# Binding the first masks of the divisors behind a projection's last exponential, and turning one adjacency mask a tile earlier, in a four-layer graph network

## The chip, the cores and the metric

The kernel runs on one core of a Trainium2 chip. The metric is the device time of one execution in microseconds (us). The engines are TensorE (PE, with its weight loads as PEld), VectorE (DVE), ScalarE (ACT), GpSimd (POOL) and SyncE (SP), which here only issues DMAs.

## The reference

N = 2708 nodes with 512 features pass four layers over one adjacency matrix `adj` (2708 x 2708, some 2% ones). Every layer adds its output to its input and normalizes each row (layer norm). Cut to what matters:

```python
# layer 0: only the first 64 neighbours of each row count
keep   = (adj > 0) & (cumsum(adj > 0, axis=1) <= 64)
xj     = leaky_relu((keep @ x) / max(keep.sum(1), 1) @ W_nb.T + b_nb)
x      = layernorm(x + leaky_relu(x @ W_line.T + b_line) + where(keep.any(1), xj, 0))
# layer 1: mean over all neighbours, joined with the node itself
x      = layernorm(x + relu(concat([x @ W_self + b_self, mean_nb(x) @ W_nb + b_nb]) @ W_comb + b_comb))
# layer 2: graph attention, 8 heads of 64
Wh     = einsum('ni,hio->hno', x, W)
e      = leaky_relu(f1[:, :, None] + f2[:, None, :], 0.2)   # f1, f2: Wh against two vectors per head
h      = softmax(where(adj > 0, e, -9e15)) @ Wh
x      = layernorm(x + heads_side_by_side(h))
# layer 3: 8 heads as in layer 2 with elu, then one head of 512 with elu, then two linear layers
```

## The kernel before, in words

The rows are cut into NT = 22 tiles of 128; the last has 20 rows. `maskT` holds the transposed adjacency of all tiles in fp8 and stays in SBUF.

**First stage (layer 0's products, L297 to L339).** A loop over t = 0 to 21 makes two products of each tile of x: one with `wnT` (kept in two parts, yH and yL) and one with `wlT` (to `r0_dram`). Between them lies the work on the adjacency: mask i is loaded by GpSimd's queue (`load_mask`, L257), counted on ScalarE (`count`, L262), cut to the first 64 on VectorE (`place`, L268 and L271), and turned (`turn`): 22 transposes on TensorE (L280) and copies with Sign to `maskT` on ScalarE (L284). Fourteen of the 22 masks (HERE = 14) are treated in this stage; one is counted in each of a part of the steps, the last at t = 18. TensorE's order in this stage is written out by `pe()`, which chains each instruction behind the one before it. `while turned < counted - (...)` sets how far the turning lags behind the counting.

**Second stage (keep @ x, L343 on).** For groups of tiles, `kept` makes kT from `maskT` on ScalarE (L350, two buffers), and TensorE multiplies (L477). The other eight masks (14 to 21) are treated beside it by the generator `other_masks`: each is loaded into one of two rooms, `spare` or `w`, and the room of mask 14 (`spare`) lies where the masks of the first stage lay. The count of mask 14 is issued on ScalarE behind the seventh kT.

**Projection (`project`, p2 and p3).** For each tile: TensorE multiplies (L642), VectorE takes columns b and dcol (L649, L647), ScalarE makes `ecol` and `ucol` by Exp (L663, L664; for the last tile in two halves, L655 and L657), VectorE scales the product into R2 (R, L671; L660 for the last tile), and `keep_v` of the tile before turns b by a transpose (L621), takes Exp (`vrow`, L622) and stores it to `v_dram`. In the steps 16 to 19 `first` makes the attention's first four e (L718), two tiles for two heads. At the end VectorE splits ecol and ucol into bf16 parts (L581 to L585, L684, L687).

**Attention (`heads_attention`, a2 and a3).** For each block of 11 tiles and pair of heads (a run, r), over the tiles j in `order`: VectorE makes e (five buffers), ScalarE makes the mask c of e in fp8 by Sigmoid (`above`, L745, eleven buffers), TensorE multiplies e (L910), and every four tiles it multiplies the masks for the divisors (`divisors`, L814). TensorE's order here is written out by `pe()` too. The accumulators `po` lie in PSUM space that the projection used.

Outside of the orders written out, a scheduler orders each engine's queue from the dependencies, so that ScalarE may take a mask between two steps of the projection. `tc.issue_after(ins)` binds the instructions traced inside it behind `ins` where they are on the engine of `ins`; it adds no wait between engines.

Of the kernel before, what the change touches and what calls it, by code (L numbers as in the profile page):

```python
# [13 lines left out]
AF = mybir.ActivationFunctionType  # L14
# [8 lines left out]
ALPHA = 0.2  # L23
# [7 lines left out]
def kernel(  # L31
# [9 lines left out]
    nc = tc.nc  # L41
    N = x.shape[0]
    NT = -(-N // P)
# [6 lines left out]
    def rows(t):  # L50
        return min(P, N - t * P)
# [101 lines left out]
    def weight():  # L153
        return weight_tile().rearrange("p k a c -> p (k a c)")[:, :KD * D].rearrange("p (k c) -> p k c", k=KD)

    def early(first, n, make):

        made = {}

        def get(i, **how):  # L160
            for j in range(len(made), min(i + first + 1, n)):
                made[j] = make(j, **how)
            return made[i]
        return get
# [36 lines left out]
    with ExitStack() as phase:  # L201
# [26 lines left out]
        def keep_y(t, n, pm):  # L228
            highs[t] = nc.scalar.copy(yH[:n, t, :], pm[:n])  # L229
            return nc.vector.tensor_sub(yL[:n, t, :], pm[:n], yH[:n, t, :].bitcast(F32))  # L230
# [57 lines left out]
        def rows_of(src):  # L288
            return early(2, NT, lambda t: fetched(src, t, rows(t)))

        with ExitStack() as ph:
            st = ph.enter_context(tc.tile_pool(name="l0a", bufs=1))
            wnT, wlT = weight(), weight2
            room = [maskT[:, G + k, :4 * D].bitcast(F32) for k in range(2 * KD)]

            xs = rows_of(x)
            xTs = early(0, NT, lambda t, order=as_it_comes: transposed(ahead, ps_tr, xs(t), rows(t), "xT", order))

            transpose_weight(room[:KD], ps_tr, wnT, l0_w_nb)
            lows = {}
            for t in range(2):
                xT = xTs(t, order=pe)
                lows[t] = keep_y(t, P, product(xT, P, wnT, 0, pe))
            transpose_weight(room[KD:], ps_tr, wlT, l0_w_line)
            b_line = bias(bcast(l0_b_line, D))
            masks = early(1, HERE, lambda i: load_mask(i, st.tile([P, N], BF16, name="m", bufs=3)))
            masks(0)
            nc.gpsimd.memset(maskT[:, NT - 1, :], 0.0)  # L310
            nc.gpsimd.memset(maskT[:, :, N:], 0.0)
            counted = turned = 0
            for t in range(NT):
                n = rows(t)
                if t > 1:
                    lows[t] = keep_y(t, n, product(xTs(t, order=pe), n, wnT, 0, pe))
                xT = xTs(t)
                if t + 1 < NT:
                    xTs(t + 1, order=pe)
                while turned < counted - (t + 1 < NT):  # L320
                    for _ in turn(turned, masks(turned), lambda: sums(BF16, (P, G, P)), pe):
                        pass
                    turned += 1
                now = counted < min(HERE, -(-(t - 1) * HERE // (NT - 5)))
                if now:
                    m, places = masks(counted), st.tile([P, N // 2], BF16, name="places", bufs=1)
                    with tc.issue_after(highs[t].ins):
                        count(counted, m)
                    with tc.issue_after(lows[t].ins):
                        place(counted, m, places, 0, 2)  # L330
                pm = product(xT, n, wlT, 1, pe)
                u = sm.tile([P, D], F32, name="u")
                nc.vector.tensor_add(u[:n], pm[:n], b_line[:n])  # L333
                low = rows_made = leaky(u[:n], u[:n])
                nc.gpsimd.dma_start(r0_dram[t * P:t * P + n, :], u[:n])
                if now:
                    with tc.issue_after(low.ins):
                        place(counted, m, places, 1, 2)
                    counted += 1  # L339
# [3 lines left out]
        with ExitStack() as ph:  # L343
# [123 lines left out]
            for i, b in enumerate(cuts):  # L467
# [19 lines left out]
                for t in ts_:  # L487
                    n = rows(t)
# [9 lines left out]
            for t in range(NT):  # L498
                n = rows(t)
# [15 lines left out]
        with ExitStack() as ph:  # L515
            st = ph.enter_context(tc.tile_pool(name="l1b", bufs=2))
            for t in range(NT):
                n = rows(t)
# [68 lines left out]
    def project(name, source, layer, v_dram, cuts, turned=None, first=None):  # L587


        w_src, w_view, _, heads = atts[layer]  # L590
# [9 lines left out]
        with ExitStack() as ph:  # L600
# [14 lines left out]
            bs, scaled = {}, {}  # L615

            def keep_v(t):
                n = rows(t)
                vrow = sm.tile([heads, P], F32, name="vrow")
                ps = ps_v.tile([P, P], F32, name="ps_v")  # L620
                nc.tensor.transpose(ps[:heads, :n], bs[t][:n, :heads], ident[:n, :n])  # L621
                nc.scalar.activation(vrow[:, :n], ps[:heads, :n], AF.Exp, scale=ALPHA - 1.0)  # L622
                nc.scalar.dma_start(v_dram[:, t * P:t * P + n], vrow[:, :n])

            for t in range(NT):
                n = rows(t)
# [21 lines left out]
                b = bs[t] = sm.tile([P, H], F32, name="b")  # L648
# [31 lines left out]
                a, z = next(c for c in cuts if c[0] <= t < c[1])  # L680
# [69 lines left out]
    blocks = list(zip(cuts[:-1], cuts[1:]))  # L750
# [1 line left out]
        oT_dram.append(dram.tile([D, (z - a) * P], F32, name=f"oT_dram{i}"))  # L752
        rc_dram.append(dram.tile([H, 12 * P], F32, name=f"rc_dram{i}"))

    def heads_attention(name, att, as_rows, meanwhile={}):

# [1 line left out]
        with ExitStack() as ph:  # L760
# [127 lines left out]
            for r, (b, h0) in enumerate(runs):  # L888
                w = att.width(b)
                parts = [(c, min(c + 4 * P, w)) for c in range(0, w, 4 * P)]  # L890
                hs = (h0, h0 + 1)
                vs = [att.load(b, h) for h in hs] if r else att.vs
                po = [ps_o.tile([P, 512], F32, name="po", tag="po") for _ in parts]
                pair = []
                if r + 1 == len(runs):
                    for j, steps in meanwhile.items():
                        todo[j] = todo.get(j, []) + steps
                for i_, j in enumerate(order):
                    if j == LAST:
                        es = [att.weights(b, h0, j, both)] * 2  # L900
                        cs = [att.above(b, h0, j, es[0])] * 2
                        if r + 1 < len(runs):
                            both = att.load_both(*runs[r + 1])
                    else:
                        es = ([att.weights(b, h, j, v) for h, v in zip(hs, vs)] if r or i_ > 1 else
                              att.early[2 * i_:2 * i_ + 2])
                        cs = [att.above(b, h, j, e) for h, e in zip(hs, es)]
                    for i, (c0, c1) in enumerate(parts):
                        for k, (h, e) in enumerate(zip(hs, es)):
                            pe(nc.tensor.matmul(po[i][HO * k:HO * k + HO, :c1 - c0], R2[:, j, h * HO:(h + 1) * HO],  # L910
                                                e[:, c0:c1], start=(i_ == 0), stop=(i_ == NT - 1)))
                    if len(pair) == 4:
                        divisors(b, pd[r % 2], pair)
                        pair = []
                    pair.append((i_, j, hs, cs))
                    for step in todo.get(i_, ()):
                        step()
                oT = sm.tile([P, 3, 512], F32, name="oT", bufs=1)
                for i, (c0, c1) in enumerate(parts):
                    nc.scalar.copy(oT[:, i, :c1 - c0], po[i][:, :c1 - c0])  # L920
                late_steps = {j: todo[j] for j in todo if j >= NT}
                todo = finish(b, h0, pd[r % 2], pair, oT, r + 1 == len(runs))
                for j, steps in late_steps.items():
                    todo.setdefault(j - NT, []).extend(steps)
                if h0 == H - 4 and b + 1 < len(att.blocks):
                    products, fold, keep = masks(b + 1, pd[r % 2])
                    for j, steps in ((12, products[:1]), (16, products[1:2]), (20, products[2:]), (NT, [fold]), (NT + 2, [keep])):
                        todo[j] = steps + todo.get(j, [])
# [195 lines left out]
    vd = [dram.tile([heads, N], F32, name=f"v_dram{i}") for i, heads in enumerate((H, H, 1))]  # L1124
    for i, source in enumerate((plain, summed)):
        with ExitStack() as ph:
            att = Weights(ph, f"a{2 + i}", blocks, vd[i])
            project(f"p{2 + i}", source, i, vd[i], blocks, first=att.first)
            heads_attention(f"a{2 + i}", att, i == 0, {
                9 + 4 * t: [lambda t=t: ready.update({t: elu_turned(None, t, t + 1)})] for t in range(3)} if i else {})  # L1130
    ph4 = fast.enter_context(ExitStack())
    att = Weights(ph4, "a4", quads, vd[2])
    lin = ph4.enter_context(tc.tile_pool(name="lin", bufs=1)).tile([P, KD * FF + KF * D + KD * 512], F32, name="lin")
    scaled = project("p4", None, 2, vd[2], quads, elu_turned)
# [327 lines left out]
```

## Time and profile before

| | |
|---|---|
| median of 3 runs | 2969.1 us (2968.95 to 2974.76) |
| profiled execution, own time | 2975.79 us |
| its span, from the first to the last instruction | 2973.9 us |
| mean granted TensorE clock | 0.995 |
| busy: TensorE / VectorE / ScalarE / GpSimd | 97% / 67% / 52% / 7% |
| Sigmoid masks L745 | 688, 1423 ns mean |
| first projection's last vrow, attention's first matmul (p2, a2) | 975.48, 975.69 us from the start |
| the same of p3, a3 | 1626.88, 1627.09 us |
| first matmul of the second stage (L477) | 217.72 us |

In the timeline, each line has the start, the duration, the engine, the line of the kernel, the operation, output and inputs, the count, and in brackets the idle time of the engine before it and what ended it. Times are from the start of the span. In the waits, the numbers are us in total, times, and the longest. In the windows, each engine has its busy us and its instructions, then come TensorE's granted clock, the DMA engines' busy share and GB/s.

### The profile page before, as it was taken

To read this page: it belongs to the slowest core of one execution; us is meant where nothing else is said; L and a number is where in the kernel's file an instruction comes from. 1 tells how busy PE (TensorE), PEld (TensorE's weight loads), DVE (VectorE), ACT (ScalarE), POOL (GpSimd) and SP (SyncE) were. 2 spreads that over 40 slices of the span, in tenths; PEclk is the share of its full clock that TensorE was granted. 3 is DMA by queue.
4 is the path that set the end of the run, shared out by engine and by line. 5 is a ranking of instruction groups with operands and counts; after the bars stand their busy time and mean duration, and the time that the engine had idled before them with its cause. 6 is when DMAs were issued, how large, how long until landed. Compare 5 with 4: busy or idle time off the path is not lost. (4 is left out here: it accounts for less than half of the span.)

```text
span 2973.9 us, 36611 instructions
## 1 busy us (share of the span) xinstructions
PE 2879.2 (97%) x14462; PEld 1605.8 (54%) x14462; DVE 1998.3 (67%) x2406; ACT 1536.7 (52%) x1775; POOL 207.9 (7%) x344
## 2 busy tenths in 40 slices
PE   8999999999999999999999999999999999999998
PEld 3447766448888343444456334434475555555555
DVE  5966637543234899999977999999963535445342
ACT  3545533113224899999966899999951000000001
POOL 1110100101110000000012000000000000000001
PEclk9999999999999999999999999999999999999999
DMA  4532426322222011111144111121061000000000
GB/s 121 122 91 57 113 87 171 130 62 92 79 74 81 21 52 46 38 45 44 32 126 147 40 40 39 41 64 37 29 160 61 4 25 14 25 14 16 15 18 24
DMA packets 121153, 185.61 MB, mean 62 GB/s; under 512 B 41741, under 2 KB 66562, under 8 KB 120972
## 3 DMA queue, kind: packets, MB, share of 16 engines
q1 hardware_dynamic: 92096, 122.09, 13.7%
q0 software_dynamic: 18160, 57.39, 6.8%
q10 hardware_dynamic: 10716, 3.69, 0.5%
q8 instruction: 116, 1.90, 0.3%
q14 instruction: 65, 0.53, 0.1%
HBM read 153.10 MB, written 44.65 MB: 66 GB/s over the span
## 5 line engine op out<-in xcount | busy, mean ns | idle before, releaser
L718 DVE SCALAR_TENSOR_TENSOR e<-v_bc,ucol,maskT 128x1408 f32<-128x1408 f32 (+3 forms) x804 | 1135.3, 1467 | 328.0 <-PE pn L1091 315.0
L745 ACT ACTIVATE c<-e,bcol 128x1300 fp8e4<-128x1300 f32 (+1 forms) x688 | 968.3, 1423 | 77.4 <-DVE e L718 33.5
L910 PE MATMUL po<-e,R 128*64 128x512 f32 (+2 forms) x4224 | 905.9, 548 | 33.4 <-DVE e L718 25.9
L910 PEld LDWEIGHTS po<-e,R 128*64 128x64 f32 x4224 | 339.8, 137 | 566.4 <-issue 397.1
L1091 PE MATMUL pn<-e,R 128*128 128x512 f32 (+1 forms) x1056 | 413.4, 542 | 0.0
L1091 PEld LDWEIGHTS pn<-e,R 128*128 128x128 f32 x1056 | 191.1, 190 | 199.2 <-issue 196.1
L1042 ACT ACTIVATE w<-pl,b 128x256 f32<-128x256 f32 (+1 forms) x88 | 41.0, 466 | 373.1 <-PE pl L1040 365.2
L477 PE MATMUL acc<-yH,kT 128*128 128x512 f32 x484 | 198.1, 409 | 6.4 <-ACT kT L350 6.4
L477 PE MATMUL acc<-yL,kT 128*128 128x512 f32 x484 | 190.1, 393 | 0.0
L528 PE MATMUL acc<-yH,mf 128*128 128x512 f32 x484 | 188.4, 389 | 0.0
L528 PE MATMUL acc<-yL,mf 128*128 128x512 f32 x484 | 188.3, 389 | 0.0
L244 PE MATMUL pm<-w,xT 128*128 128x512 f32 (+1 forms) x376 | 172.9, 603 | 14.6 <-DVE yL L230 12.1
L642 PE MATMUL pm<-w,xT 128*128 128x264 f32 (+1 forms) x704 | 166.4, 389 | 5.5 <-DVE R L671 2.4
L244 PE MATMUL pm<-weight,xT 128*128 128x512 f32 (+1 forms) x344 | 158.3, 603 | 2.7 <-DVE u L333 1.9
L1040 PE MATMUL pl<-lin 128*128 128x256 f32 (+1 forms) x704 | 154.8, 374 | 2.8 <-DVE lin L939 2.8
L120 POOL TENSOR_TENSOR ln_rs<-ln_rs,half 128x1 f32<-128x1 f32 (+1 forms) x88 | 54.2, 616 | 1449.3 <-DVE ln_rs L119 1380.8
L1065 PE MATMUL pl<-lin,w 128*128 128x512 f32 x336 | 150.8, 593 | 0.0
L1040 PEld LDWEIGHTS pl<-lin 128*128 128x128 f32 x704 | 130.4, 192 | 33.7 <-issue 15.8
L525 ACT CAST mf<-maskT 128x1024 fp32r<-128x1024 fp8e4 (+1 forms) x66 | 64.5, 978 | 156.5 <-PE acc L528 152.9
L642 PEld LDWEIGHTS pm<-w,xT 128*128 128x128 f32 (+1 forms) x704 | 128.7, 188 | 30.2 <-ACT xT L133 4.5
L229 ACT CAST yH<-pm 128x512 fp32r<-128x512 f32 (+1 forms) x43 | 25.2, 586 | 225.1 <-PE pm L244 225.1
L350 ACT ACTIVATE kT<-maskT 128x512 fp32r<-128x512 fp8e4 (+1 forms) x132 | 77.5, 593 | 117.6 <-PE acc L477 117.5
(237 smaller groups left out, 2726.2 us busy)
## 6 DMA issues: line engine op xcount, KB each, us to landing
rows<-x_dram SPq DMA_DIRECT2D x63, 256.0 KB
v_bc<-v_dram SPq DMA_DIRECT2D x16, 704.0 KB
rows<-in_x_dram SPq DMA_DIRECT2D x42, 256.0 KB
x_dram<-u POOLq DMA_DIRECT2D x42, 256.0 KB, 2.3
v_bc<-v_dram SPq DMA_DIRECT2D x16, 650.0 KB
m<-in_adj_dram POOLq DMA_DIRECT2D x13, 677.0 KB, 7.0
r_dram<-u POOLq DMA_DIRECT2D x21, 256.0 KB, 2.3
rows<-r_dram SPq DMA_DIRECT2D x21, 256.0 KB
```

The lines of the kernel that those rows point to most:

```text
L244: order(nc.tensor.matmul(pm[:n], xT[:, k, :n], w[:, k, :], start=(k == 0), stop=(k == KD - 1)))
L350: made = nc.scalar.activation(kT[:, :w], maskT[:, j, b[0] * P:b[0] * P + w], AF.Relu, scale=-1.0)
L477: nc.tensor.matmul(pa[t], kT[:, (t - b[0]) * P:(t - b[0] + 1) * P], y[:, j, :], start=(j == 0 and y is yH), stop=(j == NT - 1 and y is yL))
L525: nc.scalar.copy(mf[:, :g1 - g0, :], maskT[:, g0:g1, t * P:(t + 1) * P])
L528: nc.tensor.matmul(pa, mf[:, j - g0, :], y[:, j, :], start=(j == 0 and y is yH), stop=(j == NT - 1 and y is yL))
L642: nc.tensor.matmul(pm[a][:m, :D // 2 + heads], xT[:, k, :m], w[:, k, a, :D // 2 + heads], start=(k == 0), stop=(k == KD - 1))
L718: self.made = nc.vector.scalar_tensor_tensor(e[:, :w], v[:, :w], ucol[:, j, h:h + 1], maskT[:, j, c0:c0 + w], op0=OP.max, op1=OP.mult)
L745: nc.scalar.activation(c[:, :w], e[:, :w], AF.Sigmoid, bias=bcol[:, j, h:h + 1], scale=STEP, saturate=False)
L910: pe(nc.tensor.matmul(po[i][HO * k:HO * k + HO, :c1 - c0], R2[:, j, h * HO:(h + 1) * HO], e[:, c0:c1], start=(i_ == 0), stop=(i_ == NT - 1)))
L1040: nc.tensor.matmul(pl[:, :w], self.lin1[:, k, f * P:(f + 1) * P], h[:, k, :w], start=(k == 0), stop=(k == KD - 1))
L1065: nc.tensor.matmul(pl[:n], gT[:, f, (t - t0) * P:(t - t0) * P + n], self.lin2[:, f, :], start=(f == 0), stop=(f == KF - 1))
L1091: nc.tensor.matmul(pn[k][:, :w], R2[:, j, k * P:(k + 1) * P], e[:, :w], start=(j == 0), stop=(j == NT - 1))
```

## The change

The lag of the turning ends one step earlier: at t = 20 all counted masks are turned, where before that was at t = 21. So mask 13 is turned between the two products of tile 20 and not between those of tile 21.

`keep_v` keeps its Exp as `scaled["v"]`, so that after the projection it is that of the last tile. `project` returned the dictionary before; the caller now takes it and gives this Exp to `heads_attention` as `exps`. There the masks of the first two tiles of the first run (four of them) are issued inside `tc.issue_after(exps.ins)`. The other masks are as before.

```diff
-                while turned < counted - (t + 1 < NT):
+                while turned < counted - (t + 2 < NT):
...
-                nc.scalar.activation(vrow[:, :n], ps[:heads, :n], AF.Exp, scale=ALPHA - 1.0)
+                scaled["v"] = nc.scalar.activation(vrow[:, :n], ps[:heads, :n], AF.Exp, scale=ALPHA - 1.0)
...
-    def heads_attention(name, att, as_rows, meanwhile={}):
+    def heads_attention(name, att, as_rows, exps, meanwhile={}):
...
-                        cs = [att.above(b, h, j, e) for h, e in zip(hs, es)]
+
+                        with tc.issue_after(exps.ins) if r == 0 and i_ < 2 else nullcontext():
+                            cs = [att.above(b, h, j, e) for h, e in zip(hs, es)]
...
-            project(f"p{2 + i}", source, i, vd[i], blocks, first=att.first)
-            heads_attention(f"a{2 + i}", att, i == 0, {
+            scaled = project(f"p{2 + i}", source, i, vd[i], blocks, first=att.first)
+            heads_attention(f"a{2 + i}", att, i == 0, scaled["v"], {
```

## The prediction

> **What bounds the kernel now.** I read the page first, then the chain of waits of TensorE, then the timeline of each engine around the three places that the diff touches, and the windows there for the granted clock.
>
> ```profile
> PE 2879.2 (97%) x14462; PEld 1605.8 (54%) x14462; DVE 1998.3 (67%) x2406; ACT 1536.7 (52%) x1775; POOL 207.9 (7%) x344
> ...
> PE po L910 <- DVE e L718: 25.9, 58, 1.8
> ...
> PE acc L477 <- ACT kT L350: 6.4, 7, 3.4
> PE po L910 <- ACT vrow L622: 6.3, 2, 4.8
> ...
> PE pm L642 <- DVE R L671: 2.4, 4, 1.1
> PE pm L642 <- ACT xT L133: 2.1, 3, 1.2
> ```
>
> TensorE is busy for 97% of the span; only 2973.9 - 2879.2 = 94.7 us are idle, and an edit off TensorE pays only out of these. The diff touches the last four rows: 17.2 us idle in all, of which the two waits at L910 (4.8 and 1.5) and the 3.4 at L477 are the large ones. The timeline of ScalarE at the end of the first projection (p2), and of TensorE behind it:
>
> ```profile
> 970.85 0.27 ACT L622 ACTIVATE vrow<-ps_v 8x128 f32<-8x128 f32 x1
> ...
> 971.23 1.28 ACT L745 ACT_TABLE_LOAD   x1
> 972.52 1.47 ACT L745 ACTIVATE c<-e,bcol 128x1408 fp8e4<-128x1408 f32 x1
> 974.01 1.28 ACT L655 ACT_TABLE_LOAD   x1
> 975.30 0.16 ACT L655 ACTIVATE ecol<-pm 20x4 f32<-20x4 f32 x1
> ...
> 975.48 0.16 ACT L622 ACTIVATE vrow<-ps_v 8x20 f32<-8x20 f32 x1
> ...
> 975.69 10.18 PE L910 MATMUL po<-e,R 128*64 128x512 f32 x38 [4.78 <-ACT vrow L622]
> ```
>
> A mask (Sigmoid, L745) stands in front of the projection's last Exps. It costs a table load, itself and a table load back: 1.28 + 1.47 + 1.28 = 4.03 us of ScalarE. The attention's first matmul reuses the accumulator space that the last Exp (vrow, L622) reads, so it waits for all of it. Five masks stand so in each projection: in p2 at 949.3, 955.9, 962.7, 967.3 and 972.5, in p3 at 1604.8, 1612.1, 1617.5, 1623.3 and 1628.4. In the first stage:
>
> ```profile
> 222.68 0.42 ACT L350 ACTIVATE kT<-maskT 128x256 fp32r<-128x256 fp8e4 x1 [0.52 <-PE acc L477]
> 224.79 2.55 ACT L262 ACTIVATE spare<-spare,gate 128x2708 bf16<-128x2708 bf16 x1 [1.69 <-DMA spare<-in_adj_dram]
> ...
> 214.92 0.73 POOL L257 DMA_DIRECT2D spare<-in_adj_dram  x1 [0.99 <-PE acc L280]
> ...
> 227.79 0.50 PE L477 MATMUL acc<-yH,kT 128*128 128x512 f32 x1 [3.37 <-ACT kT L350]
> ...
> 229.00:232.20 3.20, 3.20 (x9) 2.52 (x8) 3.10 (x4) 0.84 (x2) 0.00 (x0) 0.51 0.28 84
> ```
>
> Mask 14 ("spare") is loaded only when the transposes of mask 13 (L280) have left its room, lands 9.9 us after its issue at 214.92, and its count (2.55 us) stands ahead of the next kT on ScalarE: TensorE idles 3.37 us, and the window after it (clock in the column after POOL's) runs at 0.51.
>
> **What the Trainium skill says.** "ScalarE: Activation LUTs", What ACT_TABLE_LOAD costs: about 1283 ns for the load and 1380 ns of drain per switch of set. The trace shows the 1.28 us; the next ACTIVATE starts at once behind it, and 0.02 us or less stand ahead of the load, so I price a switch at 1.28. The same page advises grouping by table set, which the second edit does. "TensorE: Matmul & The Clock Gate", Part 1: half clock after an idle window of about 3.4 us, until about as much activity. The trace agrees: 0.51 behind the 3.37 us wait, 0.50 from 975.7 to 979.0 behind the 4.78 us one, and full clock behind waits of 1.5 to 1.8 us.
>
> **Part 1, mask 13 turned at t = 20.** The test differs only at t = 20, so one turn moves: 22 transposes, in TensorE's written order 1.34 us (212.85 to 214.19), and four Sign copies on ScalarE (2.66 us). No instruction is added. The transposes come from between the two products of t = 21 to between those of t = 20: TensorE is full in both places (windows 200 to 217.7: no idle), so they cost the same; ScalarE is idle for over 6 us there (6.81 before 212.96), which hides the Signs. Mask 13's last edit on VectorE ends by 194, so nothing new is waited for at 205.7. What it brings: the transposes end at about 207, so spare's load can go on POOL's queue at about 207 instead of 214.92, past the load of w (213.22) and one store of r0 (211.13), neither of which it holds by more than its own 0.73 us. The DMA share is 0.11 from 207 to 213, so it lands by about 214 to 217. The count then follows the kT of 222.68 at once, at 223.1: **1.69 us** gone from the 3.37. A wait of 1.7 leaves the clock up (the one at 243.12, 1.66 us, does), so the 3.2 us at half clock, worth 1.6, go too: at most 3.3. What is late next is place(14) on VectorE, four parts in 8.7 us; it began at 227.94 behind an addition (L398) that waited until 227.33 for a DMA. If that addition still stands there and lands no sooner, the second group of transposes waits for the fourth part, and only 0.7 stays. The two mask loads together hold the DMA at 0.98 from 217.7 to 224.4; apart, the small loads behind them land sooner. I take **-2.5** (0 to -3.3; below zero on the cost side nothing but a swapped queue order is seen, +0.5).
>
> **Part 2, masks behind the last Exp.** The edit binds the first four masks of each stage (r = 0, two tiles, two heads); the fifth (i_ = 2, head 0), whose e is also made early (963.61), is not bound. ScalarE issues no more and no fewer Sigmoids; table loads in each stretch fall from 11 to 3 (or 5), at 1.28 each.
>
> p2: undisturbed, a tile takes TensorE 4.11 us (937.12, 941.23, 945.34 on ScalarE's side). From the tile at 953.62, three steps put the last one at 965.9 and its end near 969.5, against 970.5. Without masks the last Exp follows about 0.5 us later, as the pieces have it (dcol 0.15, ps_v 0.18, Exp 0.16): L910 starts near 970.1, 5.6 us before 975.69. But the free fifth mask, ready near 962, takes 4.03 us of ScalarE there; it delays ecol of the tile before the last but one, so R (L671) and the accumulator that the last tile needs, by some 1.4: start near 971.4, ecol (L655) at 971.2. After the start VectorE sets the pace (waits of 0.64, 0.52 and 0.52 for e): its splits (L581 to L687, 5.3 us) follow ecol, now 4.1 earlier. The half clock behind the wait was covered by that, so it is not counted again. **-4.1** (-5.6 without the fifth mask; -0.9 if ecol's second half falls behind one mask, as in p3, where the third group of divisors comes 0.85 us later after the start than in p2).
>
> p3: the mask at 1604.76 held xT (1.24 at 1608.89), another R (0.43 at 1621.72); the last Exp was 1.5 late. Together 3.2 at best; with the fifth mask near 1616 delaying the last tile by 1.3, **-1.8** (-3.2 to 0).
>
> The added wait: behind Exp, one load and four masks take 1.28 + 4 x 1.47 = 7.2 us. Their divisors are read only after four tiles, over 12 us after the start. The five e buffers are the tighter use: the sixth e needs the first freed by TensorE (start + 2.7) and its mask (start + 2.8); the next masks end at +4.2, +5.7, +7.1, the matmuls at +3.2, +6, +6.4, and VectorE at 1.68 per e asks no sooner. Hidden.
>
> **Sum.** -2.5 - 4.1 - 1.8 = -8.4. The profiled execution took 2975.8 (span 2973.9 and 1.9 around it), so 2967.4 in its terms; it stands 6.7 above the median of 2969.1, from which I forecast **2960.7**. The stages behind are bound by TensorE, so nothing gives it back.
>
> **Rivals.** (1) *The free fifth mask takes the place of the bound ones.* If e5 comes 6 us later, its mask stands before the last ecol and costs the same 4.03: p2 keeps about 1, p3 nothing, and with the 0.7 of part 1 it is -1.7: 2967.4. For it: the fifth already stands there now (972.52 and 1628.35). Against: e5 came right behind e4 in both stages. (2) *Slower: a row of masks ahead of the second half of ecol and ucol (L655, L657 of the last tile).* That half waits for R (L660) by 0.37 us, and the row could start in this gap. It then ends 8.6 us after the start; L660, first in VectorE's queue ahead of the splits and of e6, is late as much; e6 at start + 14 instead of + 5.6 starves TensorE by 8.4 in each stage: +4.3 and +6.6, with -2.5 for part 1, 2977.5. It decides once more than two masks stand there. Against: p3 shows one mask slipping in (1628.35) and ecol right behind it. (3) The edits change nothing, because the order of the queues is not theirs to set: excluded for the turn, which lies in TensorE's written order; for the masks the bind is an order on one engine.
>
> **Numbers.** A difference of 0.2%, 5.9 us, is about what a measurement of this kernel can tell. The forecast has a chance of 0.62, with its own range of 2957 to 2963; rival 1 and milder sums of the low ends (0.7 + 3.3 + 0.5 = 4.5) 0.25; rival 2 0.12. Faster 0.62, same 0.26, slower 0.12. The range goes from all best ends (-3.3 - 5.6 - 3.2 = -12.1, 2957, and a little for scatter) up to 2969.5, leaving out mainly rival 2.
>
> **What would show it.** After: one Sigmoid or none before the last vrow in p2 and p3, L910's wait for vrow below 1 us in both, and full clock there; no gap of 1.7 before the count of spare, and the L477 wait near 1.7 at full clock. Wrong if a mask stands between the last tile's products and the last vrow, if L910's waits for e grow by more than 2 us per stage, or if place of mask 14 still starts near 228.

## The result, and the profile after

The changed kernel takes 2965.54 us (median of 20 runs, 2960.45 to 2971.01) where the kernel before takes 2970.22 (20 runs, 2967.92 to 2974.76): ratio **0.9981** (0.9975 to 0.9988). In a second set beside the experiments it was 2962.77 (10 runs) against 2970.35 (18 runs): ratio **0.9974** (0.9965 to 0.9983). So it is faster by 0.19% and 0.26%, right at the 0.2% that the forecast took as the edge; the medians lie 4.7 and 7.6 us apart. (The ratios and their 95% intervals are given as recorded; a ratio is not exactly the quotient of its two medians, which is 0.9984 in the first set.) The forecast was 2960.7, in a range from a little under 2957 up to 2969.5.

The two spans (2973.9 before, 2965.8 after) differ by 8.1 us, but the kernel before, profiled a second time, spanned 2964.4, so a span is no measure here. Stretches, the times between two fixed instructions of one execution, are a better one. First comes the first profile after, then a table of stretches. The page after, its first part (busy us, share, instructions):

```profile
PE 2877.5 (97%) x14462; PEld 1604.3 (54%) x14462; DVE 1997.9 (67%) x2406; ACT 1514.1 (51%) x1759; POOL 205.7 (7%) x344
```

TensorE's waits after (us in total, times, longest):

```profile
PE po L912 <- DVE e L718: 28.0, 60, 2.7
...
PE acc L477 <- ACT kT L350: 4.5, 7, 1.6
...
PE po L912 <- ACT vrow L622: 1.7, 2, 0.9
...
PE pm L642 <- ACT xT L133: 1.0, 2, 0.7
PE pm L642 <- DVE R L671: 0.9, 2, 0.7
```

(L912 is the L910 of before.) The wait for vrow fell from 6.3 to 1.7 and the longest kT wait from 3.4 to 1.6; ScalarE has 16 instructions fewer (1775 to 1759), the table loads saved. But the waits for e rose from 25.9 to 28.0, with a longest of 2.7: something was given back. It was given back in a2, where they rose from 9.4 to 11.7 (in a3: 16.5 and 16.3). The end of p2 in ScalarE's timeline, after:

```profile
968.51 0.18 ACT L622 ACTIVATE vrow<-ps_v 8x20 f32<-8x20 f32 x1
968.84 1.28 ACT L745 ACT_TABLE_LOAD   x1
970.13 1.47 ACT L745 ACTIVATE c<-e,bcol 128x1408 fp8e4<-128x1408 f32 x1
...
971.62 1.28 ACT L655 ACT_TABLE_LOAD   x1
972.91 0.17 ACT L655 ACTIVATE ecol<-pm 20x4 f32<-20x4 f32 x1
```

No mask stands before the last vrow any more. One, and only one, slipped in between it and the second half of ecol (L655), with a switch of tables on either side. VectorE's timeline beside it:

```profile
968.72 0.27 DVE L660 TENSOR_TENSOR R<-pm,ecol 20x128 f32<-20x128 f32 x1
971.63 1.69 DVE L718 SCALAR_TENSOR_TENSOR e<-v_bc,ucol,maskT 128x1408 f32<-128x1408 f32 x1 [2.64 <-ACT c L745]
973.35 0.48 DVE L660 TENSOR_TENSOR R<-pm,ecol 20x128 f32<-20x128 f32 x2
...
977.04 1.67 DVE L718 SCALAR_TENSOR_TENSOR e<-v_bc,ucol,maskT 128x1408 f32<-128x1408 f32 x1
```

and TensorE's:

```profile
968.74 7.31 PE L912 MATMUL po<-e,R 128*64 128x512 f32 x36 [0.86 <-ACT vrow L622]
978.76 1.07 PE L912 MATMUL po<-e,R 128*64 128x512 f32 x2 [2.71 <-DVE e L718]
980.48 6.63 PE L912 MATMUL po<-e,R 128*64 128x512 f32 x22 [0.65 <-DVE e L718]
```

VectorE has nothing to do for 2.64 us: the sixth e, first in its queue, waits for a buffer that the first mask frees, and everything else stands behind it. Then L660 and the first splits come in one piece, the seventh e not before 977.04, and TensorE, 5 us earlier at its start than before, waits 2.71 and 0.65 us.

In a3 VectorE has the same gap, 2.52 us, but there it is not new. Before the change one mask already slipped in front of the second half of ecol in p3, and VectorE's timeline had

```profile
1629.70 3.28 DVE L718 SCALAR_TENSOR_TENSOR e<-v_bc,ucol,maskT 128x1408 f32<-128x1408 f32 x2 [2.52 <-PE po L910]
```

There it was TensorE, and not a mask, that freed the buffer last.

In the first stage after, GpSimd's timeline has

```profile
208.35 0.71 POOL L257 DMA_DIRECT2D spare<-in_adj_dram  x1 [3.50 <-PE acc L280]
```

ScalarE's

```profile
223.67 2.54 ACT L262 ACTIVATE spare<-spare,gate 128x2708 bf16<-128x2708 bf16 x1
```

and TensorE's

```profile
226.66 0.49 PE L477 MATMUL acc<-yH,kT 128*128 128x512 f32 x1 [1.53 <-ACT kT L350]
```

Spare's load goes out 10 us before the first L477 (218.3) in place of 2.8, and its count has no bracket: ScalarE was not idle before it.

TensorE's stretches, in us, each from the timeline of one execution and from start to start. The columns are:

- L477: the first L477 to the last.
- p2: p2's first product (L642) to the first product of its last tile.
- start a2: from there to the first attention matmul.
- to L797: from there to the attention's first masks product, L797.
- p3's end: the product of p3's fourth tile before its last to that of its last; then "start a3" and "to L797" as for p2.

| kernel | L477 | p2 | start a2 | to L797 | p3's end | start a3 | to L797 |
|---|---|---|---|---|---|---|---|
| before | 278.6 | 87.1 | 8.9 | 41.3 | 18.3 | 5.4 | 42.2 |
| before_again | 276.9 | 87.1 | 8.9 | 41.3 | 18.3 | 5.4 | 42.2 |
| after | 275.5 | 86.0 | 4.9 | 43.0 | 16.2 | 4.9 | 42.9 |
| after_again | 275.0 | 86.0 | 4.9 | 43.0 | 16.2 | 4.9 | 42.9 |
| turn_only | 275.8 | 87.1 | 8.9 | 41.3 | 18.3 | 5.4 | 42.2 |
| turn_held | 279.5 | 87.1 | 8.9 | 41.3 | 18.3 | 5.4 | 42.2 |
| bind_only | 279.4 | 86.0 | 4.9 | 43.0 | 16.2 | 4.9 | 42.9 |
| bind_half | 275.0 | 86.0 | 4.9 | 40.3 | 16.2 | 4.9 | 40.2 |

What the bind sets repeats to 0.1 us. What the change doesn't touch scatters: over all profiles, the first L477 began at 212.9 to 218.7, and p3 up to its last tile took 90.6 to 96.0.

### The profile page after: what moved, and what is told of

Its sections match the earlier page's. It is cut to its first block, busy times and chain, and to the rows that moved or that the text cites. A ratio compares the mean times of both kernels' runs of the same rounds, so it can differ in the third digit from the quotient of the medians.

```text
span 2965.8 us, 36608 instructions
## 1 busy us (share of the span) xinstructions
PE 2877.5 (97%) x14462; PEld 1604.3 (54%) x14462; DVE 1997.9 (67%) x2406; ACT 1514.1 (51%) x1759; POOL 205.7 (7%) x344
## 5 line engine op out<-in xcount | busy, mean ns | idle before, releaser
L912 PE MATMUL po<-e,R 128*64 128x512 f32 (+2 forms) x4224 | 906.2, 549 | 30.9 <-DVE e L718 28.0
L912 PEld LDWEIGHTS po<-e,R 128*64 128x64 f32 x4224 | 340.3, 137 | 563.8 <-issue 396.7
L477 PE MATMUL acc<-yH,kT 128*128 128x512 f32 x484 | 197.3, 408 | 4.5 <-ACT kT L350 4.5
L477 PE MATMUL acc<-yL,kT 128*128 128x512 f32 x484 | 189.2, 391 | 0.0
L642 PE MATMUL pm<-w,xT 128*128 128x264 f32 (+1 forms) x704 | 165.6, 388 | 3.0 <-ACT xT L133 1.0
L642 PEld LDWEIGHTS pm<-w,xT 128*128 128x128 f32 (+1 forms) x704 | 127.8, 187 | 27.7 <-ACT xT L133 3.6
```

The lines of the kernel that those rows point to most:

```text
L477: nc.tensor.matmul(pa[t], kT[:, (t - b[0]) * P:(t - b[0] + 1) * P], y[:, j, :], start=(j == 0 and y is yH), stop=(j == NT - 1 and y is yL))
L642: nc.tensor.matmul(pm[a][:m, :D // 2 + heads], xT[:, k, :m], w[:, k, a, :D // 2 + heads], start=(k == 0), stop=(k == KD - 1))
```

## The experiments

**The kernel before, again (before_again).** No edit.

> The kernel before, unchanged, profiled a second time and timed against itself. The two profiled executions differ by 8.1 us (2975.79 and 2967.70) where the medians differ by 4.68 (2970.22 and 2965.54). Theory: the difference by stretches is the change's and the first profile of before was a late one among its own runs (2967.9 to 2974.8). Expected: ratio 1.000, span 2967 to 2973; TensorE's stretch from the first L477 to its last 278.4 if the 3.37 us wait and the half clock behind it return, down to about 276 if the wait or the half clock is chance; the wait at L910 for vrow 4.8 and 1.5 again. Rival: the gaps of the three places are chance of that execution and are not found again.

Measured: ratio 1.0001 (0.9992 to 1.0009), span 2964.4. The stretches are those of the first profile except L477, 276.9. Its wait, in TensorE's timeline:

```profile
222.53 0.50 PE L477 MATMUL acc<-yH,kT 128*128 128x512 f32 x1 [2.91 <-ACT kT L350]
```

The wait is back, 2.91 in place of 3.37, but the clock stayed at 1.00 behind it this time. The rival falls: all three gaps are found again. The half clock of the first stage does not come in every execution, and the span is lower than I expected.

**The turn alone.**

```diff
-                while turned < counted - (t + 1 < NT):
+                while turned < counted - (t + 2 < NT):
```

> The turn of mask 13 at t = 20 alone, the masks bound nowhere. Theory: spare's load goes on GpSimd's queue near 208, its count stands behind the seventh kT without a wait, TensorE's wait for kT is 1.6 in place of 3.37 at full clock, and the stretch from the first L477 to its last is 275.3 in place of 278.4; all else as before, L910 waits 4.8 and 1.5 for vrow; about -2 to -3 us in the profile, 0.9990 to 0.9995 in the timed runs. Rival: the turn only moves the wait on to place(14), and the stretch is within 0.7 of before.

Measured: L477 275.8, its wait 1.55 at full clock, the other stretches as before; ratio 0.9991 (0.9982 to 0.9999), 2967.29 against 2970.07. As the theory has it.

**The turn with the load held back.** On top of turn_only:

```diff
-                nc.gpsimd.dma_start(r0_dram[t * P:t * P + n, :], u[:n])
+                stored = nc.gpsimd.dma_start(r0_dram[t * P:t * P + n, :], u[:n])
...
-                    load_mask(i, m)
+                    with tc.issue_after(stored.ins) if i == HERE else nullcontext(): load_mask(i, m)
```

> As turn_only, with the load of mask 14 (spare) held on GpSimd's queue behind the last store of r0, near 220 in place of 208; the transposes stay at t = 20. Theory (the load is what the turn brings): the count waits for a landing near 227, TensorE's wait for kT is 4 to 6 us, and the half clock is back. Rival (the moved transposes and Signs themselves bring it): the wait stays near 1.6 to 2.

Measured, in the timelines of GpSimd,

```profile
217.30 0.75 POOL L257 DMA_DIRECT2D spare<-in_adj_dram  x1
```

ScalarE,

```profile
223.78 2.55 ACT L262 ACTIVATE spare<-spare,gate 128x2708 bf16<-128x2708 bf16 x1 [2.48 <-DMA spare<-in_adj_dram]
```

and TensorE:

```profile
226.78 0.79 PE L477 MATMUL acc<-yH,kT 128*128 128x512 f32 x1 [4.15 <-ACT kT L350]
```

This execution's first L477 is at 215.0, so the load is 2.3 behind it. The wait is 4.15, the half clock is back (0.50 from 226.7 to 230), and the stretch is 279.5, with the transposes where the change has them. So with the load late, the moved transposes bring nothing: what the turn brings is the earlier load. (Timed once only, 2971.67.)

**The bind alone.** The changed kernel with the first line of turn_only undone.

> The bind of the first four masks alone, mask 13 turned at t = 21 as before. Theory: p2's tile of step 16 to the third group of divisors takes 67.4 us in place of 70.7 (start of L910 5 earlier, 1.7 given back to waits for e), p3's same stretch 76.5 in place of 78.3; the first stages as before; -5 us in the profile, 0.9980 to 0.9987 in the timed runs. Rival: the gain at the start of L910 is taken back in full by waits for e, and both stretches are within 1 us of before.

Measured: p2 and the start of a2 as in the changed kernel (86.0 + 4.9 + 43.0 against 87.1 + 8.9 + 41.3, -3.4), p3's tail and the start of a3 too (16.2 + 4.9 + 42.9 against 18.3 + 5.4 + 42.2, -1.9); 2965.22 against 2970.07, ratio 0.9987 (0.9979 to 0.9994), at the edge of what was expected. The theory stands.

**The changed kernel, again.**

> The changed kernel once more, profiled and timed. Theory: the stretches that the change touches are set by its order and come out as in its first profile (first L477 to last 275.5, last tile of p2 to the first L912 4.9, from there to the first masks product 43.1; p3's last tile, start and masks product 602.1, 4.9 and 42.9), while the time up to the first L477 is chance and lies anywhere from 212 to 219. Ratio to before 0.9975 to 0.9988. Rival: the stretches vary by as much as the sum, 8 us, is apart from the median's 4.7.

Measured: the row in the table, 217.0 to the first L477. The stretches repeat, so they are the order's and not one execution's. The ratio, 0.9974 (0.9965 to 0.9983), is a hair below what was expected; its interval and the first set's overlap from 0.9975 to 0.9983.

**The masks behind the second half too (bind_half).**

```diff
-                            nc.scalar.activation(ucol[at, t, i::2], d2, AF.Exp, scale=1.0 - ALPHA)
+                            scaled["h"] = nc.scalar.activation(ucol[at, t, i::2], d2, AF.Exp, scale=1.0 - ALPHA)
...
-                        with tc.issue_after(exps.ins) if r == 0 and i_ < 2 else nullcontext():
+                        with tc.issue_after(exps[0].ins) if r == 0 and i_ < 2 else nullcontext(), tc.issue_after(exps[1].ins) if r == 0 and i_ < 2 else nullcontext():
...
-            heads_attention(f"a{2 + i}", att, i == 0, scaled["v"], {
+            heads_attention(f"a{2 + i}", att, i == 0, (scaled["v"], scaled["h"]), {
```

> As the changed kernel, with the four masks bound behind the second half of the last tile's ucol (L657) as well as behind vrow. Theory: the first mask slips in ahead of ecol's second half because only vrow is named; with both named, two table loads of each stage go, L660 and the splits on VectorE come some 4 us earlier, the waits for e behind the start (2.7 + 0.65 + 0.53 in a2, 2.6 + 0.16 + 0.38 + 0.52 in a3) fall under 1.5, and the stretch from the start to the first masks product is 40 to 41.3 in place of 43.1 and 42.9: 4 to 5 us less than the changed kernel in all. Rival: the sixth e waits for the first mask anyway (the row of masks holds the e buffers), and the stretches stay at 42.5 to 43.

Measured, VectorE's timeline in a2:

```profile
968.37 0.49 DVE L660 TENSOR_TENSOR R<-pm,ecol 20x128 f32<-20x128 f32 x2 [0.24 <-ACT ecol L655]
...
971.35 1.69 DVE L718 SCALAR_TENSOR_TENSOR e<-v_bc,ucol,maskT 128x1408 f32<-128x1408 f32 x1
```

and TensorE's:

```profile
967.88 8.16 PE L912 MATMUL po<-e,R 128*64 128x512 f32 x38 [0.86 <-ACT vrow L622]
976.79 2.79 PE L912 MATMUL po<-e,R 128*64 128x512 f32 x12 [0.75 <-DVE e L718]
980.24 1.93 PE L912 MATMUL po<-e,R 128*64 128x512 f32 x8 [0.67 <-DVE e L718]
```

VectorE's idle time is 0.24 in place of 2.64, the first splits are done while the first mask runs, and the stretches are 40.3 and 40.2, 2.7 less in each stage. That is more than the change had given back (1.7 in a2 and 0.7 in a3), because in a3 the gap was there before the change. 2959.05 against 2970.35, ratio **0.9955** (0.9943 to 0.9967): faster than the kernel before by more than the changed kernel is, whose median in the same set is 3.7 us higher.

**The count of mask 14 earlier (count0).**

```diff
-                        for _ in range(5):
+                        for _ in range(0):
```

> As the changed kernel, with the count of mask 14 traced at the first step of the second stage in place of the sixth (five yields left out). Theory: spare now lands near 215, while ScalarE is idle until the third kT at 219.6, so that the count (2.55) fits there and the last 1.6 us of TensorE's wait for kT go too: first L477 to last about 273.9 in place of 275.5. Rival: the seven other masks move with it and collide elsewhere in the stage, or yH of the last tile waits behind the count, and the stretch is the same or longer.

Measured: the count ran at 211.90, before the first L477 (215.6), and the wait behind it is gone. But the stretch is 275.3, and other waits stand in the stage. TensorE's timeline has

```profile
246.61 0.50 PE L477 MATMUL acc<-yH,kT 128*128 128x512 f32 x1 [0.94 <-ACT kT L350]
```

and two more of 0.95 at 292.52 and 338.43. Each comes right after the count of a later mask (243.41, 289.32 and 335.23); in the changed kernel the counts of these masks cost 0.27 us at most. Ratio 0.9973 (0.9962 to 0.9984), as the changed kernel in the same set. The first half of the theory held, the sum did not: the rival.

**Both (both0).**

> bind_half and count0 in one. Theory: their gains lie in stretches apart and add: 6 to 7 us less than the changed kernel, ratio to before 0.995 to 0.9965. Rival: no more than the better of the two.

Measured: 40.3 and 40.2 again, L477 276.3, ratio 0.9957 (0.9944 to 0.997). No more than bind_half: the rival, as after count0 it had to be. (Its ratio lies in the range expected for the sum, but so does bind_half's own; the stretches decide.)

**More masks ahead of the second half (late2, late4).** Two and four masks there in place of one. For late4, besides handles that keep the instructions:

```diff
+                        if r == 0 and i_ == 1: tc.add_manual_dep(exps[1].ins, att.mask.ins.name, mybir.DependencyInfo(mybir.DependencyClass.NoSync, mybir.DependencyReason.DATA), reason="order")
```

(`exps[1]` is the second half's ecol, `att.mask` the mask made last; late2 has `i_ == 0`.)

> As the changed kernel, with the second half of ecol and ucol (L655, L657) put behind the second mask in place of the first. Rival 2 of the prediction: each mask more ahead of that half makes VectorE and TensorE later, by 1.5 us or more in each stage (start of L912 to first masks product 44.5 or more in place of 43.0). Theory now: the pace behind the start is set by what stands ahead of the e's on VectorE, not by how late the half is. VectorE's queue here has two e (the sixth and seventh) ahead of L660 and two more inside the splits, where the changed kernel has one and one behind all of the first splits; so TensorE's longest wait for e falls under 1.5 and the stretch comes to 41 to 42.5.

> The same with the half behind the fourth mask: the row of four masks of rival 2 in full. Rival 2: 8.4 us lost in each stage against an undisturbed start, the stretch at 48 or more. Theory now: VectorE's queue has four e ahead of L660, each released in time by TensorE and by its own mask, and the splits that follow are needed only later; the stretch comes to 40 to 41.5, near bind_half's 40.3, and the ratio to before is 0.995 to 0.997.

Measured: stretches to L797 of 42.7 and 42.9 (late2; timed once, 2961.9) and 42.4 and 42.3 (late4); late4 2957.37 against 2970.81, ratio 0.9959 (0.9943 to 0.9974). VectorE's timeline in late4:

```profile
967.06 6.47 DVE L718 SCALAR_TENSOR_TENSOR e<-v_bc,ucol,maskT 128x1408 f32<-128x1408 f32 x4 [2.64 <-ACT c L745]
973.56 0.48 DVE L660 TENSOR_TENSOR R<-pm,ecol 20x128 f32<-20x128 f32 x2
```

and TensorE's:

```profile
964.17 10.52 PE L913 MATMUL po<-e,R 128*64 128x512 f32 x50 [0.86 <-ACT vrow L622]
977.62 4.27 PE L913 MATMUL po<-e,R 128*64 128x512 f32 x10 [2.93 <-DVE e L718]
```

(L913 is the L912 of the changed kernel.) Both theories missed the stretch. Rival 2's starving does not come, even with the whole row: the scheduler queued four e ahead of L660, so the queue that rival 2 assumed, with L660 in front of e6, was not built. But the four e in time do not bring 40.3 either. The idle 2.64 is the same as with one mask, and so, to 0.6 us, is the stretch; TensorE's wait of 2.93 only moved two e later.

Why the order matters so little shows in the windows of the stretch in a2, of the kernel before, the changed one, bind_half and late4 in turn (start and end, length, busy us of PE, PEld, DVE, ACT and POOL, granted clock, DMA share, GB/s):

```profile
975.69:1017.02 41.33, 39.64 (x246) 15.98 (x250) 40.76 (x47) 32.52 (x26) 0.23 (x1) 0.95 0.06 18
968.74:1011.77 43.03, 39.14 (x246) 15.68 (x250) 39.98 (x47) 41.28 (x33) 0.23 (x1) 0.96 0.13 35
967.88:1008.20 40.32, 37.88 (x247) 15.16 (x250) 39.76 (x47) 38.38 (x31) 0.23 (x1) 1.00 0.12 36
964.17:1006.61 42.44, 39.21 (x246) 15.76 (x250) 39.52 (x47) 40.79 (x33) 0.84 (x1) 0.96 0.12 34
```

VectorE's work, the third of the busy times, is 39.5 to 40.8 us in all four, and the stretch is this work plus the time that VectorE stands idle: 0.57, 3.05, 0.56 and 2.92 us. So VectorE sets the pace here, and what counts is how long it idles, not in which order it works: 3.05 - 0.56 = 2.5 us of idle time account for most of the 43.0 - 40.3 = 2.7 us between the changed kernel and bind_half. ScalarE is nearly as busy, but behind the gap no wait of VectorE or TensorE for it is seen in the changed kernel's stretch. The half clock (0.96 on the mean) doesn't set the stretch either: TensorE still waits for e 28 us behind the start, so it has caught up by then.

Late4's timed ratio is near bind_half's first, where the stretches say 4.2 us more in all; in its own set bind_half is 1.9 us faster (below). What makes up the rest is not shown; p3 up to its last tile took only 90.6 in late4's profile, the lowest of all, so chance may play a part.

**bind_half, again.**

> bind_half once more, against late4 and before on one chip: stretches 40.3 and 40.2 again, ratio 0.9943 to 0.9967. Rival: its first times were a good draw, and the ratio falls to that of the changed kernel, 0.9974 to 0.9981.

Measured: 40.3 and 40.2, 2955.49 (5 runs) against 2970.81 (9), ratio **0.9948** (0.9935 to 0.9962). It holds.

## Why the prediction was right or wrong

**Part 1, -2.5.** Right, and in the main by its own steps: the turn cost TensorE nothing, the load went out at once, the count lost its wait, and TensorE's wait came to 1.5 to 1.6. The addition L398 that might have held place(14) started earlier (225.64 in place of 227.33), as it should when the two mask loads no longer meet; no run tests that cause by itself. Measured: L477 278.6, 276.9 and 279.4 without the turn, 275.0 to 275.8 in the table's four executions with it: 1.1 to 4.4, and 2.9 between the means. The half clock of 1.6 was counted as always there before; it came in two of the three executions without the turn, so that the sum is right on the mean and not in each execution.

**Part 2, p2, -4.1.** The start at L910 came 5.1 earlier (1.14 in the products and 3.92 behind the last tile). I had 5.6 undisturbed, less some 1.4 for the fifth mask. The step "the free fifth mask ... takes 4.03 us of ScalarE there" failed: it never came, in no profile of any kernel with the bind. The first mask slipped in late, the others followed it. A kernel that binds only the first two masks, or the first six, comes out as the same program as the changed one, instruction for instruction (built, not run): here the bind of the first two already holds the row. Rival 1 falls with it.

Then 1.7 was given back on the way to the first masks product. The step that failed here is "The added wait ... VectorE at 1.68 per e asks no sooner. Hidden." The buffer's times were right (freed by the first mask at about start + 2.8; the sixth e began 2.9 after the start), but VectorE asked at start + 0.3, because its splits, which I had placed at once behind the start, stood behind an ecol that a mask delayed. I had given this case 0.85, from p3 before; it costs 1.7 here. By the windows above, that is 2.5 us more of idle time on VectorE less 0.8 us of its work, which is now done before the start. One of the prediction's own signs of being wrong showed with it: the waits for e in a2 grew by 2.3 us, more than the 2 allowed. And "nothing gives it back" was right of the stages behind, but not of the attention's start, where VectorE sets the pace. Net -3.4.

**Part 2, p3, -1.8.** Measured: -2.14 in the last tiles, -0.44 at the start, +0.72 behind it: -1.86. The size is luck, two wrong terms that in part cancel: the fifth mask (1.3) did not come, and the give-back (0.72) was not in the sum. This give-back is not that of a2: VectorE's gap was there before, and what is new is 0.6 us more of its work that falls behind the earlier start (39.96 us in the stretch, 39.38 before).

**The sum, -8.4.** The stretches give -2.9 - 3.4 - 1.9 = -8.2, close to the forecast, but by other terms: no fifth mask, and a give-back. The timed medians give -4.7 in one set and -7.6 in the other, with intervals in the ratio of about -3.6 to -7.4 and -5.0 to -10.4 us. The sum lies in the second and just outside of the first. The base was low by 1.1 (three runs, 2969.1; twenty, 2970.2). What else separates the first set from the stretches stays open; nothing in the profiles takes the gain back, and the untouched parts scatter by 5 us and more from one execution to the next.

**The chances.** 0.62 stood on faster by over 0.2%; the first ratio is 0.9981, a hair inside the edge, the second beyond it. The time lies in the range in both. Of rival 2, the one on the slower side, late4 put the row of four masks on the chip: the stretch is 0.6 us less than with one mask, not 8.4 more. What remains untested is its queue, with L660 ahead of e6.

## What to carry to other kernels

A bind that clears a path should name everything that the path's next consumer needs: here "behind the last exponential" left half of one tile's exponentials outside, a mask with two table loads went into the gap, and naming that half too took 5.4 us more out of the two stretches (3.7 us between the timed medians of one set). When an early start is won on the bounding engine, look at once at the engine that feeds it: behind the start of a2, where VectorE had as much to do as TensorE (about 40 us each), nearly each us that it idled made the stretch longer, in whatever order its work was queued. And before a gain of a few us is read from two spans, profile the same kernel twice and compare stretches: the spans of one kernel lay 9.5 us apart, the stretches at the ends of its projections agreed to 0.1.

## What the runs showed of the hardware

The half clock (a granted clock of about 0.5) came behind waits shorter than I had thought. In the changed kernel, the two waits of 2.71 and 0.65 us at the start of a2, with 1.07 us of matmuls between them, were followed by half clock, as two windows show (start and end, length, busy us of PE, PEld, DVE, ACT and POOL, granted clock, DMA share, GB/s):

```profile
976.00:980.40 4.40, 1.12 (x4) 0.19 (x2) 4.30 (x10) 4.40 (x4) 0.00 (x0) 1.00 0.00 0
980.50:983.50 3.00, 3.00 (x9) 1.18 (x11) 3.00 (x4) 3.00 (x3) 0.00 (x0) 0.52 0.00 0
```

TensorE was busy for 1.12 of 4.4 us, and the clock went to 0.52. A single wait can do it too: 2.66 in late2 and 2.93 in late4, both in a2, were followed by 0.50. The idle window of about 3.4 us that the prediction took from the Trainium skill ("TensorE: Matmul & The Clock Gate", Part 1) is therefore no safe bound here: no single wait was that long, and the measurement decides. In bind_half, with waits of 0.75 and 0.67 at the same place, it stayed at 1.00. But before_again's single wait of 2.91 at L477 brought no half clock, and bind_only's of 3.11 did. So in these runs a wait of 2.7 to 3 us sometimes cost half the clock for some 3 us and once did not; its length alone doesn't decide, and what does is not shown.
